# Summing the weighted values of a graph-attention block: accumulating transposes against an fp32 matmul with a stationary identity

## The chip, the cores and the metric

The kernel runs on one core of one Trainium2 chip. The metric is the device time of an execution in microseconds (us), as the median of several runs.

## The reference

Four graph layers are applied in sequence to x (3327 nodes, 256 features, fp32) under an adjacency matrix adj (3327 x 3327, int32, about 0.5% ones). Layer 0 is a simple attention over all nodes. Layers 1, 2 and 3 are the same block with their own weights, 8 heads of 32 features:

```python
qkv = layer_norm(x, g1, be1) @ w_qkv
qkv = qkv.reshape(n, 3, HEADS, HEAD_DIM)
q, k, v = (qkv[:, 0], qkv[:, 1], qkv[:, 2])
scores = jnp.einsum('nhd,mhd->hnm', q, k) * SCALE
scores = jnp.where((adj != 0)[None, :, :], scores, -jnp.inf)
attn = jax.nn.softmax(scores, axis=-1)
out = jnp.einsum('hnm,mhd->nhd', attn, v).reshape(n, DIM)
x = x + out @ w_proj + b_proj
h2 = layer_norm(x, g2, be2)
return x + jax.nn.gelu(h2 @ w1 + b1) @ w2 + b2
```

What matters here is the weighted sum `out`: a node has only some 16 neighbours, and out is the sum over them of (share of the head) times (value row).

## The kernel before, in words

**Layer 0 and the lists.** The first 420 us or so compute layer 0, turn the adjacency into a list of neighbours for each node, and sort the nodes by their number of neighbours into 26 blocks of 128. CAPS gives the slots (places for neighbours) of each block, from 34 for block 0 down to 9 for block 25, 430 in all. None of this is touched by the change.

**A layer.** `layer(L)` runs once for each of layers 1 to 3 under a schedule that is written out by hand: the order in which the Python code issues instructions is the order in each engine's queue. Blocks come in the order 23, 22, ... 0, 24, 25 (ORDER). A block's slots are cut into groups of 3 or 4 (`cuts`); one pass of the inner loop, a *turn*, handles one group. There are 354 turns in three layers. In a turn:

- `gather` issues, up to three groups ahead, one indirect DMA per slot on POOL's queue (L775). It brings for each of the 128 nodes of the block the key and the value row of one neighbour, 2 KB, into a slot tile `sl` (12 tiles of four slots).
- `scores` multiplies the keys by q on DVE (L789) and sums over each head (L790). q lies in a PSUM tile `qp`, which ACT fills in `place_q` (L768). After a block's last group, `exps` and, a turn later, `shares` form the softmax.
- `turn()` advances the *tails* by one step each. A tail is a Python generator for a chunk of two blocks (the last two blocks are chunks of their own): projection (L676), residual, layer norm, the two MLP matmuls (L700, L713) with gelu (L704) between them, and, in layers 1 and 2, the next layer's norm and q, k, v (`qkv_rows`, L182 to L189), whose rows go out by DMA on SP's queue (L739, L740). A number given by `yield` says after how many turns the generator goes on. `hidden` lets only one tail at a time into the MLP.
- `values` works on the block before the current one. DVE multiplies the value half of a group in place by the shares (L822), and PE then adds the group's slots up.

**How the slots are added up.** A slot holds 128 nodes in partitions and 256 features along the free axis, and the projection needs features in partitions. Each slot is therefore turned by two PE transposes (L825), each with the slot's data as the weights and the identity as the moving operand, and all transposes of a block accumulate into one PSUM tile `po` (2 x 128 columns): the sum is already turned. A matmul of zeros (L812) opens the accumulation for both halves at once. When the last group is in, ACT copies po into `oT` (L831), and `part` starts the chunk's tail at the next turn once both of its blocks are there. Behind that copy, in ACT's queue, stands `place_q` for the next block.

**Buffers.** [...]four in the ring `gen` for everything in the tails, two for po, two for qp. In SBUF the pool `work` has two buffers for each tag; the tag `kv` belongs to the k/v rows that `qkv_rows` copies out.

Of the kernel before, what the change touches and what calls it, by code (L numbers as in the profile page):

```python
# [8 lines left out]
FP = mybir.dt.float32  # L9
BF = mybir.dt.bfloat16  # L10
# [8 lines left out]
P = 128  # L19
N = 3327  # L20
D = 256
# [38 lines left out]
CHUNKS = [ORDER[k:k + 2][::-1] for k in range(0, NB - 2, 2)] + [[NB - 2], [NB - 1]]  # L60
# [3 lines left out]
def kernel(ctx: ExitStack, tc: tile.TileContext, ins, out: bass.AP):  # L64
    nc = tc.nc

    def wt(L, name):
        return ins[f"L{L}_gnn_{name}"]

    const = ctx.enter_context(tc.tile_pool(name="const", bufs=1))  # L70
# [3 lines left out]
    ident = const.tile([P, P], FP, name="ident")  # L74
# [2 lines left out]
    nc.vector.tensor_copy(ident_bf, ident)  # L77
    ones = const.tile([P, P], FP, name="ones")
    nc.vector.memset(ones, 1.0)
    zeros_bf = const.tile([1, 2 * P], BF, name="zeros_bf")  # L80
    nc.vector.memset(zeros_bf, 0.0)
    mhalf = const.tile([P, 4], FP, name="mhalf")
    nc.vector.memset(mhalf, -0.5)

# [18 lines left out]
    def load_wq(L):  # L103
        t = wq_pool.tile([P, 2, 3 * D], FP, tag="wq", name=f"wq{L}")
        nc.sync.dma_start(t, wt(L, "w_qkv").rearrange("(c p) n -> p c n", p=P))
        return t
# [87 lines left out]
    def node_rows(b):  # L194

        if b not in nodes_:
            nodes_[b] = lists.tile([P, NODE], FP, tag="node", bufs=NODES, name=f"node_{b}")
        nc.gpsimd.indirect_dma_start(
            out=nodes_[b], out_offset=None, in_=node_dr[:, :],
            in_offset=bass.IndirectOffsetOnAxis(ap=perm[:, b:b + 1], axis=0))  # L200
# [34 lines left out]
    with ExitStack() as st, tc.manual_schedule():  # L235
# [17 lines left out]
        o = 0  # L253
# [33 lines left out]
        for L in LAYERS:  # L287
            o = 16 * (L - 1)
            for k, name in ((0, "g1"), (2, "be1"), (4, "g2"), (6, "be2"), (8, "b1")):
                n = wt(L, name).shape[0] // P  # L290
                nc.sync.dma_start(cols[o + k:o + k + n, :], wt(L, name).rearrange("(c p) -> c p", p=P))
        for L in LAYERS:
            for k, name in enumerate(("b_proj", "b2")):
                r = 2 * (L - 1) + k
# [99 lines left out]
        for i in range(NB):  # L394
            r = ROWS[i]
# [195 lines left out]
        for i in range(NB + 1):  # L591
# [6 lines left out]
            for part, k0 in enumerate(range(0, NB, 8)):  # L598
# [15 lines left out]
                if i:  # L614
                    for k in range(k0, k0 + kn):
                        nc.tensor.matmul(pa[:, :3 * H0 + 1], aTs[i - 1][:, k, :], hs[:, k, :],
                                         start=(k == 0), stop=(k == NB - 1))
# [6 lines left out]
            if i:  # L624
                f, j = in_fin[i - 1]
# [14 lines left out]
    with ExitStack() as st:  # L640
        keep = st.enter_context(tc.tile_pool(name="keep", bufs=1))
        wts = st.enter_context(tc.tile_pool(name="wts", bufs=1))
        work = st.enter_context(tc.tile_pool(name="work", bufs=2))
        slots = st.enter_context(tc.tile_pool(name="slots", bufs=SLOTS))
        ps_g = st.enter_context(tc.tile_pool(name="ps2_g", bufs=4, space=PSUM))
        ps_o = st.enter_context(tc.tile_pool(name="ps2_o", bufs=2, space=PSUM))
        ps_q = st.enter_context(tc.tile_pool(name="ps2_q", bufs=2, space=PSUM))

        def gen(name):
            return ps_g.tile([P, 512], FP, tag="g", name=name)  # L650

        x_sb = keep.tile([P, NB, D], FP, name="x_sb")
        def node_x(b):
            nc.scalar.copy(x_sb[:, b, :], nodes_[b][:, :D])

        def load_weights(L):
            w = {}
            for name, c, n in (("w_proj", 2, D), ("w1", 2, FF), ("w2", 8, D)):
                w[name] = wts.tile([P, c, n], FP, tag=name, name=f"{name}_{L}")
                nc.sync.dma_start(w[name], wt(L, name).rearrange("(c p) n -> p c n", p=P))  # L660
            return w
# [88 lines left out]
        class Attend:  # L750
# [51 lines left out]
            def shares(self):  # L802
                S = self.S
                scs = self.sc[:, :S, :]
                sm = work.tile([P, HEADS], FP, tag="sm", name=f"sm_{self.tag}")
                nc.vector.tensor_reduce(sm, scs.rearrange("p s h -> p h s"), AX.X, ALU.add)
                nc.vector.reciprocal(sm, sm)

                self.pw = self.qp[:, :LW * HEADS].rearrange("p (s h) -> p s h", h=HEADS)
                nc.vector.tensor_mul(self.pw[:, :S, :], scs, sm[:, None, :].to_broadcast([P, S, HEADS]))  # L810
                self.po = ps_o.tile([P, 2, P], FP, tag="po", name=f"po_{self.tag}")
                nc.tensor.matmul(self.po.rearrange("p c r -> p (c r)"), zeros_bf[:, :P], zeros_bf,  # L812
                                 start=True, stop=False)

            def values(self, oT, j):

                g = self.vdone
                a, z = self.cuts[g]
                n = z - a
                t = self.tiles[g]  # L820
                vv = t[:, :n, D:2 * D].rearrange("p s (h d) -> p s h d", h=HEADS)
                nc.vector.tensor_mul(vv, vv, self.pw[:, a:z, :, None].to_broadcast([P, n, HEADS, HD]))  # L822
                for k in range(n):
                    for c in range(2):
                        nc.tensor.matmul(self.po[:, c, :], t[:, k, D + c * P:D + (c + 1) * P], ident,  # L825
                                         is_transpose=True, start=False,
                                         stop=(a + k == self.S - 1 and c == 1))
                self.vdone += 1
                if self.vdone < len(self.cuts):
                    return False  # L830
                nc.scalar.copy(oT[:, :, j * P:(j + 1) * P], self.po)  # L831
                return True

        place = {b: (m, j) for m, blocks in enumerate(CHUNKS) for j, b in enumerate(blocks)}
        tails = []
        hidden = []

        def turn():

            for e in list(tails):  # L840
                e[0] -= 1
                if e[0] <= 0:
                    e[0] = next(e[1], None)
                    if e[0] is None:
                        tails.remove(e)

        def layer(L):
            w = load_weights(L)
            wqn = load_wq(L + 1) if L < LAYERS[-1] else None
            att = [Attend(L, b) for b in ORDER]  # L850
            todo = [(a, g) for a in att for g in range(len(a.cuts))]
            turns = len(todo)
            held = 0
            sent = 0
            oTs = {}
            left = [len(c) for c in CHUNKS]
            first = L == LAYERS[0]
            if first:
                for b in ORDER[:EARLY]:
                    node_rows(b)  # L860
                    node_x(b)
            att[0].load_q()
            att[0].place_q()
            att[1].load_q()
            before = None

            def part(a):

                m, j = place[a.b]
                if m not in oTs:  # L870
                    oTs[m] = work.tile([P, 2, 2 * P], FP, tag="oT", name=f"oT_{L}_{m}")
                if a.values(oTs[m], j):
                    left[m] -= 1
                    if not left[m]:
                        tails.append([1, tail(L, w, wqn, CHUNKS[m], oTs.pop(m))])

            now = 0
            for k, a in enumerate(att):
                n = len(a.cuts)
                if k + 2 < NB:  # L880
                    att[k + 2].load_q()
                for g in range(n):
                    if first and g == 0:
                        if k + EARLY < NB:
                            node_rows(ORDER[k + EARLY])
                        if EARLY <= k + 2 < NB:
                            node_list(ORDER[k + 2])
                            node_x(ORDER[k + 2])
                    while sent < turns and held < SLOTS and sent - now <= AHEAD:
                        todo[sent][0].gather(todo[sent][1])  # L890
                        sent += 1
                        held += 1
                    a.scores(g)
                    if g == n - 1:
                        a.exps()
                    turn()
                    if before is not None:
                        if g == 0:
                            before.shares()
                        goal = -(-len(before.cuts) * (g + 1) // max(n - 1, 1))  # L900
                        while before.vdone < min(goal, len(before.cuts)):
                            part(before)
                            held -= 1
                            if before.vdone == len(before.cuts) and k + 1 < NB:
                                att[k + 1].place_q()
                    elif g == n - 1:
                        att[1].place_q()
                    now += 1
                before = a
            before.shares()  # L910
            while before.vdone < len(before.cuts):
                part(before)
                turn()
            while tails:
                turn()
# [194 lines left out]
```

## Time and profile before

| | |
|---|---|
| Median of 3 runs | 2417.78 us (2409.95 to 2418.01) |
| The profiled execution's own time | 2978.47 us |
| Its span | 2976.6 us |
| Mean granted TensorE clock in it | 0.737 |
| Busy, of the span | PE 60%, DVE 59%, POOL 48%, PEld (weight loads) 46%, ACT 26% |
| DMA | 453.04 MB, mean 152 GB/s; POOL's queue 350.26 MB |

PE is TensorE's matmul side, PEld its weight loads, which overlap with it; DVE is VectorE, ACT ScalarE, POOL GpSimd, SP SyncE. L825 is line 825 of the kernel before. A group line gives line, engine, operation, output<-inputs, shapes and count; after the bar the busy time, the mean length of one in ns, and then the idle time of the engine just ahead of them with what ended it. "issue" is time in which an engine waited for nothing that the profile shows. Durations come from the one profiled execution, which took 561 us longer than the median of the timed runs.

### The profile page before, as it was taken

The page shows a single profiled execution, that of the slowest core. Times are in us where ns is not written, and L with a number is a line of the kernel's source. Part 1 is how long each engine was busy: PE and PEld are TensorE (multiplying, and loading weights), DVE is VectorE, ACT ScalarE, POOL GpSimd, SP SyncE. Part 2 cuts the span into 40 slices and gives each one's busy share as a digit, 9 for nine tenths or more (in the row PEclk, how much of TensorE's full clock was granted, in tenths as well). Part 3 has the DMA queues.
Part 4 walks back from the last instruction along what each step waited for, and adds up shares of the span by engine and source line. Part 5 has one row for each costly group of instructions (what it writes and reads, how often), then busy time and mean ns, then how long its engine had stood idle before and what let it go on. Part 6 is the DMA issues. An engine that isn't in the chain of part 4 may idle for free.

```text
span 2976.6 us, 26066 instructions
## 1 busy us (share of the span) xinstructions
PE 1773.0 (60%) x8346; PEld 1360.5 (46%) x8346; DVE 1769.4 (59%) x3214; ACT 776.9 (26%) x1564; POOL 1426.4 (48%) x1614
## 2 busy tenths in 40 slices
PE   7767632555675556662566665576815656555656
PEld 6545412443454444542445554455614534444545
DVE  6767646655566677715544576657436646665573
ACT  5677410222322222230122221222301221111112
POOL 0221346554445556325544456556164655665651
PEclk9888755677787777785777767778956767667777
DMA  6556275555445556435554456555174554655550
GB/s 237 186 173 196 61 137 167 151 152 148 132 138 164 160 165 181 122 131 161 148 149 132 128 172 187 165 171 171 48 232 120 163 161 129 177 165 157 169 157 24
DMA packets 165082, 453.04 MB, mean 152 GB/s; under 512 B 37711, under 2 KB 64985, under 8 KB 161609
## 3 DMA queue, kind: packets, MB, share of 16 engines
q0 software_dynamic: 107104, 350.26, 41.0%
q1 hardware_dynamic: 57468, 100.88, 11.1%
q8 instruction: 69, 1.13, 0.2%
q14 instruction: 77, 0.63, 0.1%
q10 hardware_dynamic: 364, 0.13, 0.0%
HBM read 410.86 MB, written 40.29 MB: 152 GB/s over the span
## 4 chain that ended last, share of the span: by engine, by line
PE 22%; another core or an unknown queue 11%; issue 10%; DVE 9%; POOL 3%; ACT 3%; DMA 2%; DVEq 0%; POOLq 0%; ACTq 0%
PE pd L713 6%; PE pu L700 6%; PE po L825 4%; POOL sl L775 3%; DVE sl L822 2%; DVE sl L789 2%; DMA sl<-kv,idx 2%; PE pp L676 2%; PE pk L182 2%; DVE sc L790 1%; PE pq L187 1%; DVE st_f L129 1%; DVE x_sb L679 1%; ACT L704 0%
## 5 line engine op out<-in xcount | busy, mean ns | idle before, releaser
L775 POOL DMA_INDIRECT sl<-kv,idx x1290 | 1232.9, 956 | 585.3 <-issue 366.6
L825 PE MATMUL po<-ident,sl 128*128 128x128 f32 x2580 | 482.8, 351 | 543.5 <-DVE sl L822 335.8
L789 DVE TENSOR_TENSOR sl<-sl,qp 128x1024 f32<-128x1024 f32 (+1 forms) x354 | 396.3, 1119 | 561.7 <-ACT qp L768 399.7
L825 PEld LDWEIGHTS po<-ident,sl 128*128 128x128 f32 x2580 | 403.7, 183 | 610.8 <-DVE sl L822 375.8
L700 PE MATMUL pu<-fT,w 128*128 128x256 f32 (+1 forms) x1344 | 345.0, 411 | 116.6 <-issue 93.4
L790 DVE TENSOR_REDUCE sc<-sl 128x32 f32<-128x1024 f32 (+1 forms) x354 | 398.2, 1125 | 17.4 <-DVE sl L789 3.0
L822 DVE TENSOR_TENSOR sl<-sl,qp 128x1024 f32<-128x1024 f32 (+1 forms) x354 | 389.1, 1119 | 4.0 <-DVE qp L810 1.0
L713 PE MATMUL pd<-w,gT 128*128 128x256 f32 x1248 | 324.7, 417 | 100.6 <-ACT gT L704 88.1
L700 PEld LDWEIGHTS pu<-fT,w 128*128 128x128 f32 x1344 | 273.8, 219 | 173.2 <-issue 109.0
L713 PEld LDWEIGHTS pd<-w,gT 128*128 128x128 f32 x1248 | 255.4, 210 | 197.2 <-ACT gT L704 92.7
L182 PE MATMUL pk<-wq,hT 128*128 128x512 f32 x312 | 192.7, 751 | 69.8 <-issue 48.5
L704 ACT ACTIVATE gT<-pu,pv 128x256 f32<-128x256 f32 (+1 forms) x336 | 133.0, 457 | 385.5 <-PE pu L700 164.2
L831 ACT COPY oT<-po 128x256 f32<-128x256 f32 x78 | 29.0, 372 | 754.7 <-PE po L825 359.6
L719 DVE TENSOR_TENSOR x_sb<-x_sb,pd 128x512 f32<-128x512 f32 (+1 forms) x42 | 27.2, 647 | 317.8 <-PE pd L713 247.1
L136 POOL TENSOR_TENSOR rsig_f<-rsig_f,mhalf 128x2 f32<-128x2 f32 (+1 forms) x42 | 29.4, 700 | 383.9 <-DVE rsig_f L132 383.7
L182 PEld LDWEIGHTS pk<-wq,hT 128*128 128x128 f32 x312 | 68.2, 242 | 132.0 <-issue 98.2
L187 PE MATMUL pq<-wq,hT 128*128 128x256 f32 x312 | 90.5, 417 | 61.3 <-ACT kvr L184 50.3
L187 PEld LDWEIGHTS pq<-wq,hT 128*128 128x128 f32 x312 | 67.1, 217 | 115.7 <-issue 55.4
L622 DVE MAX8 cand<-abf 128x8 f32<-128x256 bf16 x338 | 116.6, 411 | 1.9
L676 PE MATMUL pp<-w_proj,oT 128*128 128x256 f32 x312 | 102.1, 481 | 23.2 <-ACT oT L831 20.1
L162 PE MATMUL pn_f<-ident,xn_f 128*128 128x128 f32 x156 | 40.3, 395 | 92.7 <-ACT xn_f L152 69.0
L136 POOL TENSOR_TENSOR rsig_h<-rsig_h,mhalf 128x2 f32<-128x2 f32 (+1 forms) x28 | 19.4, 694 | 157.6 <-DVE rsig_h L132 122.5
(220 smaller groups left out, 1972.8 us busy)
## 6 DMA issues: line engine op xcount, KB each, us to landing
a<-in_adj_dram SPq DMA_DIRECT2D x25, 1663.5 KB
sl<-kv,idx POOLq DMA_INDIRECT x1290
kv<-kvr SPq DMA_DIRECT2D x78, 256.0 KB
q<-qr SPq DMA_DIRECT2D x52, 128.0 KB
q<-q SPq DMA_DIRECT2D x52, 128.0 KB
w<-in_L_gnn_w_dram SPq DMA_DIRECT2D x6, 1024.0 KB
node<-x SPq DMA_DIRECT2D x26, 128.0 KB
node<-qr SPq DMA_DIRECT2D x26, 128.0 KB
```

The costliest lines, as they stand in the source:

```text
L182: nc.tensor.matmul(pk, hT[:, c, :], wq[:, c, D:], start=(c == 0), stop=(c == 1))
L187: nc.tensor.matmul(pq[:, :D], hT[:, c, :], wq[:, c, :D], start=(c == 0), stop=(c == 1))
L622: nc.vector.max(out=cand[:, 8 * m:8 * m + 8], in_=ab3[:, m, :])
L676: nc.tensor.matmul(pp[:, j, :], oT[:, c, j * P:(j + 1) * P], w["w_proj"][:, c, :], start=False, stop=(c == 1 and j == n - 1))
L700: nc.tensor.matmul(pu[:, a, :n * P], w["w1"][:, c, f * P:(f + 1) * P], fT[:, c, :n * P], start=(c == 0), stop=(c == 1))
L704: nc.scalar.activation(gT[:, f0 + a, :n * P], pu[:, a, :n * P], AF.Gelu_apprx_tanh, bias=pv[:, L - 1, 8 + f:9 + f])
L713: nc.tensor.matmul(pd[:, j, :], gT[:, f, j * P:(j + 1) * P], w["w2"][:, h * FH + f, :], start=False, stop=(h == 1 and f == FH - 1 and j == ...
L775: nc.gpsimd.indirect_dma_start(out=t[:, k - a, :w], out_offset=None, in_=kv_dr[self.L][:, :], in_offset=bass.IndirectOffsetOnAxis(ap=idx[: ...
L789: nc.vector.tensor_mul(kq, kq, self.qp[:, None, :D].to_broadcast([P, n, D]))
L790: nc.vector.tensor_reduce(self.sc[:, a:z, :], kq.rearrange("p s (h d) -> p s h d", h=HEADS), AX.X, ALU.add)
L822: nc.vector.tensor_mul(vv, vv, self.pw[:, a:z, :, None].to_broadcast([P, n, HEADS, HD]))
L825: nc.tensor.matmul(self.po[:, c, :], t[:, k, D + c * P:D + (c + 1) * P], ident, is_transpose=True, start=False, stop=(a + k == self.S - 1 ...
```

## The change

The slots of a block are first added up unturned, and the sum is turned once. A matmul with the identity as the stationary operand copies its moving operand to its output; with two slots as the moving operand (2 x 256 = 512 columns) it adds two slots into one PSUM bank, the even ones on the left half and the odd ones on the right. A group of four takes two such matmuls, a group of three one of 512 columns and one of 256. The matmul of zeros goes, since the first matmul of a block opens the accumulation. After a block's last group ACT copies the 512 columns to SBUF (`so`, in the tag `kv`). A new generator `turned_out` joins the tails: at the next turn four transposes turn so and add its two halves into a bank of `gen`, a turn later ACT copies that into oT, and if the block completes its chunk the chunk's tail follows after another turn.

```diff
-    zeros_bf = const.tile([1, 2 * P], BF, name="zeros_bf")
-    nc.vector.memset(zeros_bf, 0.0)
...
-                self.po = ps_o.tile([P, 2, P], FP, tag="po", name=f"po_{self.tag}")
-                nc.tensor.matmul(self.po.rearrange("p c r -> p (c r)"), zeros_bf[:, :P], zeros_bf,
-                                 start=True, stop=False)
+                self.po = ps_o.tile([P, 2 * D], FP, tag="po", name=f"po_{self.tag}")
...
-                for k in range(n):
-                    for c in range(2):
-                        nc.tensor.matmul(self.po[:, c, :], t[:, k, D + c * P:D + (c + 1) * P], ident,
-                                         is_transpose=True, start=False,
-                                         stop=(a + k == self.S - 1 and c == 1))
+                for k in range(0, n, 2):
+                    m = min(2, n - k)
+                    nc.tensor.matmul(self.po[:, :m * D], ident, t[:, k:k + m, D:2 * D],
+                                     start=(a + k == 0), stop=(a + k + m == self.S))
                 self.vdone += 1
                 if self.vdone < len(self.cuts):
                     return False
-                nc.scalar.copy(oT[:, :, j * P:(j + 1) * P], self.po)
+                self.so = work.tile([P, 2 * D], FP, tag="kv", name=f"so_{self.tag}")
+                nc.scalar.copy(self.so, self.po)
                 return True
+
+            def turned_out(self, oT, j, then):
+                po = gen(f"pt_{self.tag}").rearrange("p (c r) -> p c r", c=2)
+                for m in range(2):
+                    for c in range(2):
+                        o = m * D + c * P
+                        nc.tensor.matmul(po[:, c, :P], self.so[:, o:o + P], ident, is_transpose=True,
+                                         start=(m == 0 and c == 0), stop=(m == 1 and c == 1))
+                yield 1
+                nc.scalar.copy(oT[:, :, j * P:(j + 1) * P], po[:, :, :P])
+                if then:
+                    yield 1
+                    yield from then
...
                     left[m] -= 1
-                    if not left[m]:
-                        tails.append([1, tail(L, w, wqn, CHUNKS[m], oTs.pop(m))])
+                    oT = oTs[m] if left[m] else oTs.pop(m)
+                    tails.append([1, a.turned_out(oT, j, None if left[m] else tail(L, w, wqn, CHUNKS[m], oT))])
```

## The prediction

> **What bounds the kernel now.** I read the page first (engine totals, clock slices, chain, groups), then the wait totals, then the timeline of a stretch inside layer 2. On the page:
>
> ```profile
> PE 1773.0 (60%) x8346; PEld 1360.5 (46%) x8346; DVE 1769.4 (59%) x3214; ACT 776.9 (26%) x1564; POOL 1426.4 (48%) x1614
> ...
> PEclk9888755677787777785777767778956767667777
> ...
> PE 22%; another core or an unknown queue 11%; issue 10%; DVE 9%; POOL 3%; ACT 3%; DMA 2%; DVEq 0%; POOLq 0%; ACTq 0%
> ...
> L775 POOL DMA_INDIRECT sl<-kv,idx x1290 | 1232.9, 956 | 585.3 <-issue 366.6
> L825 PE MATMUL po<-ident,sl 128*128 128x128 f32 x2580 | 482.8, 351 | 543.5 <-DVE sl L822 335.8
> ```
>
> No engine is full and the chain has no owner: 21% of it has no releaser (unknown queue, issue). That share is about 613 us; the profiled execution took 2978.5 us (span 2976.6), 560.7 over the median 2417.78. I take that idle to be mostly absent from the timed runs, so I add differences to 2417.78 and trust durations, not gaps.
>
> The timeline (start, length, engine, line, count) gives the real paces:
>
> ```profile
> 1486.95 0.96 POOL L775 DMA_INDIRECT sl<-kv,idx  x1 [0.30 <-issue]
> 1488.22 0.96 POOL L775 DMA_INDIRECT sl<-kv,idx  x1 [0.30 <-issue]
> ...
> 1493.30 0.34 PEld L182 LDWEIGHTS pk<-wq,hT 128*128 128x128 f32 x1 [0.52 <-issue]
> 1494.15 0.34 PEld L182 LDWEIGHTS pk<-wq,hT 128*128 128x128 f32 x1 [0.52 <-issue]
> ```
>
> ```profile
> 1502.75 1.04 PE L825 MATMUL po<-ident,sl 128*128 128x128 f32 x8
> ...
> 1504.06 0.19 PEld L182 LDWEIGHTS pk<-wq,hT 128*128 128x128 f32 x1 [0.24 <-issue]
> 1504.48 0.19 PEld L182 LDWEIGHTS pk<-wq,hT 128*128 128x128 f32 x1 [0.24 <-issue]
> ...
> 1525.94 1.97 PE L825 MATMUL po<-ident,sl 128*128 128x128 f32 x8 [1.97 <-DVE sl L822]
> ```
>
> The reader is to see two things. POOL issues one gather (one slot) every 1.26 us, whatever else stalls. And PE has two speeds: a transpose every 0.109 us at full clock, (1.04 - 0.27)/7, and 0.213 at half clock, (1.97 - 0.48)/7; a 512-column fp32 pass every 0.43 or 0.86 us. The same starts in the trace give 0.216 or 0.427 for a 256-column pass. The mean granted clock is 0.737.
>
> Per block of S slots, outside the layer ends: **POOL** 1.26 S + 0.7 (L136, half a pair's two). **DVE** 0.92 S + 4: L789, L790 and L822 total 1187 us over 1290 slots, softmax pieces 1.8, half a pair's tail 2.2; layer 1 has some 3 more for lists. **PE** at full clock 0.218 S + 11.1: per pair of blocks 32 passes each of L700 and L713 and 8 of L676 at 0.216, four transposes (16.0 us), and for layers 1 and 2 the next q/k/v, 5.6 us; half of that, plus the zeroing matmul L812 at 0.3. At S = 18 this is POOL 23.4, DVE 20.6, PE 15.0. Adding the largest of the three over 78 blocks gives 1708 us at full clock, 1723 at 0.8. With 423 us before the first gather (read from its start) and three layer ends without gathers of about 75 us (1243 to 1318 us is the first), that is 2355 to 2370, 2% under the median. So the gather queue sets the time inside a layer, with DVE and PE close behind in narrow blocks; a serial tail sets it at the ends.
>
> How PE gets onto the path is in the wait totals (total, times, longest):
>
> ```profile
> DVE sl L789 <- ACT qp L768: 399.7, 31, 26.1
> ACT oT L831 <- PE po L825: 359.6, 46, 17.8
> POOL sl L775 <- PE po L825: 83.7, 24, 12.1
> ```
>
> ACT stands in L831 until PE has finished a block's po; the next block's q (L768) is queued behind it, and DVE's scores wait for q. Slots also come free only when PE has read them.
>
> **What the Trainium skill says.** "FP8 and Floating Point Precision", TensorE Precision Notes: true fp32 takes four passes. The trace agrees in time: L700 issues 672 matmuls and shows 1344 records, and 256 columns take 2 x 0.216 us. Transposes have one record each. "TensorE: Matmul & The Clock Gate", Part 1: the clock is half or full, set by activity in windows of about 3.4 us; the trace's clock steps only between 0.5 and 1.0. The same page, Part 4, says that transpose mode does not count as activity; here the clock rises at 1234.6 us after transposes alone since 1230.2, so I don't count on real matmuls waking it.
>
> **The change part by part.**
> 1. *po.* Removed: 2580 transposes, 2580 x 0.109 = 281 us at full clock. Added: 228 groups of four slots take two 512-column matmuls each, 126 groups of three take one and one of 256 columns. At two passes: (456 + 126) x 2 = 1164 passes x 0.429 = 499, and 252 x 0.216 = 54; together 554. Per slot 0.43 instead of 0.218. The trace has no matmul with ident as fp32 weights over a strided pair of slots; the nearest row is L182. Low end: one pass, 277 us, nothing gained or lost. High end: the 0.19 us weight load not covered by the pass before, +1416 x 0.19 = 269. I take two passes, loads covered, as in L182. **+273 us of PE.**
> 2. *Zeroing* (L812, 78 x 0.31) goes: -24 us PE.
> 3. *turned_out*: 4 x 78 transposes x 0.109 = +34 us PE. ACT's copy out of po grows from 0.37 to 0.59 us (L184's shape): +0.22 ahead of the next q; the second copy, 0.37 x 78 = 29 us, runs a turn later. ACT is 26% busy, so apart from the 0.22 this is covered. Queued behind the wait for the turning transposes on ACT are gelu and exp; the transposes have had a turn by then.
> 4. *tail* starts two turns later. Inside a layer the gathers cover that. At the end nothing does.
> 5. *Buffers.* so shares the two kv buffers with L184; it waits for a row write issued a turn before, and in the trace such packets are done 2 to 3 us after issue, so I put it at nothing, upper bound 1.5 us a block, 117 us. pt takes one more of the four gen banks per block: no row prices it; between nothing and the same bound. SP and POOL issue nothing new.
>
> PE per block becomes 0.43 S + 11.2; over three layers 1074 to 1358 us at full clock. **Inside a layer** what counts is where this passes POOL and DVE. S = 11: 15.9 against 14.6; S = 18: 18.9 against 23.4, hidden. Redoing the sum of maxima: +7 us at full clock, +34 at 0.87, +80 at 0.8, +151 at 0.74. The timed clock isn't shown; I expect about 0.8 before and somewhat more after, since PE idles less: **+45**. **At a layer end** block 0's 34 values ran at DVE's pace, 1230.2 to 1241.9 = 11.7 us; 34 passes of 0.429 take 14.6, about 18 with the first 6.8 us at half clock: +6. The last two blocks' 19 slots add 2, their copies and turns 2, the two late turns 2 to 6: **13 a layer, 39 in all**. Sum +84, or 2978.5 + 84 = 3063 for a profiled execution if its idle stayed, and **2500 us** on the median.
>
> **Rivals.**
> - *PE becomes the bound throughout.* Clock 0.74 before and after: +151 +39, or 2608. For: 0.737 in the profile. Against: that clock contains the long unexplained idle.
> - *Hidden.* Clock near full: +7, ends smaller than I think, 2427. For: POOL's steady 1.26. Against: the ends have no gathers to hide behind.
> - *Faster: the clock.* Denser PE work keeps it full where it now drops to half. From 0.74 (sum 1741) to 1 (1715) is -26; with ends at full clock and the zeroing gone, 2395. It decides if the mean clock rises by 0.2 or more. Against: transposes already wake it.
> - *The turn waits.* so or pt holds ACT 1 to 1.5 us a block ahead of q: +117 at most, with half of part 1, about 2545.
> - *One pass only* for the new matmul: then PE is level and only the tail's two turns remain, 2425, counted with "hidden".
>
> **How the numbers follow.** Forecast 50%; PE bound 18%; turn waits 10%; hidden (with one pass) 11%; faster 11%. A measurement of this kernel tells about 0.5% from no change (2406 to 2430). Faster 0.11, same 0.11, slower 0.78. The range 2405 to 2615 leaves out most of the faster case and the top of the PE-bound one.
>
> **What would show it.** Right: po with some 1416 passes of 0.43/0.86 us, PE busy up by 280 us or more at an equal clock, L831's successor waiting longer for po, longer pauses of POOL at layer ends. A profiled execution may even lose part of its idle, as PE issues fewer instructions; the timed runs decide. Wrong: half as many passes; a clock well above 0.8; or POOL's gathers still 1.26 apart through narrow blocks.

## The result, and the profile after

The kernel with the change takes **2483.98 us** (median of 4 runs, 2481.66 to 2490.44) against 2415.81 for the kernel before beside it: a ratio of **1.029 [1.0262, 1.0318]**, or +68 us. Forecast were 2500 us and +84.

The profile of before that the prediction reads holds some 560 us of idle that these runs don't have: on one of the chips used here the unchanged kernel takes some 2969 us (2949 to 2990 in all its runs), with a similar idle inside the layers, and elsewhere 2404 to 2418. So the traces are compared against a second profile of before (experiment e1: 2415.22 us, span 2413.4), which is free of it. Its page:

```profile
PE 1647.3 (68%) x8346; PEld 1290.9 (53%) x8346; DVE 1775.3 (74%) x3214; ACT 782.3 (32%) x1564; POOL 1423.6 (59%) x1614
...
PEclk9888876568887888796778889878957878877777
...
PE 26%; DVE 21%; DMA 15%; POOL 12%; issue 10%; ACT 1%; DVEq 0%; POOLq 0%; ACTq 0%
...
L825 PE MATMUL po<-ident,sl 128*128 128x128 f32 x2580 | 471.5, 346 | 531.3 <-DVE sl L822 530.5
```

And the page of the changed kernel (profiled execution 2490.44 us, span 2488.7). Most of its lines stand two lower than in before: the gathers are L773 (before L775), the power for the norms L134 (L136), the MLP L698 and L711 (L700 and L713), q's copy L766 (L768). New are the summing matmuls L822, the copy L828, the turning transposes L837 and the second copy L840.

```profile
PE 1860.2 (75%) x7416; PEld 1203.1 (48%) x7416; DVE 1775.8 (71%) x3213; ACT 828.5 (33%) x1648; POOL 1424.1 (57%) x1614
...
PEclk9888876689989989996989999899968988888889
...
PE 37%; DVE 16%; issue 13%; POOL 10%; DMA 8%; ACT 2%; DVEq 0%; POOLq 0%; ACTq 0%
...
L773 POOL DMA_INDIRECT sl<-kv,idx x1290 | 1230.2, 954 | 418.2 <-issue 318.3
L822 PE MATMUL po<-sl,ident 128*128 128x512 f32 (+1 forms) x1416 | 727.3, 656 | 408.2 <-DVE sl L818 360.2
```

Fewer PE instructions (7416 for 8346) are busy for longer (1860 us for 1647) although the mean granted clock rose from 0.794 to 0.872. DVE and POOL do what they did, and ACT is busy for 46 us more, with the added copies. PE's share of the chain goes from 26% to 37%.

**Where the time went.** The start of each gather on POOL cuts the trace into parts: a layer runs from its first to its last gather, and its end from there to the next layer's first gather (in layer 3 to the end of the span). The sums are worked out from those starts; us, layers 1, 2, 3:

| | inside the layers | their ends | before the first slot's gather |
|---|---|---|---|
| before (e1) | 605.1, 577.1, 593.2 | 70.8, 71.4, 68.2 | 427.6 |
| after | 620.2, 591.7, 597.0 | 87.1, 86.4, 78.4 | 427.9 |
| difference | +15.1, +14.6, +3.8 = **+33.5** | +16.3, +15.0, +10.2 = **+41.5** | +0.3 |

Together +75, which is the difference of the spans (2488.7 - 2413.4).

**Inside a layer, which blocks?** Layer 2 is cut where block 11, the first of the wider ones, starts its gathers. Each line: window, its length, busy time (instructions) of the engines, granted clock, DMA share, GB/s. Before (e1): narrow blocks, wide blocks, end of the layer.

```profile
1103.50:1322.20 218.70, 139.34 (x622) 109.60 (x623) 162.43 (x233) 60.75 (x117) 163.38 (x173) 0.73 0.74 229
1322.20:1655.10 332.90, 256.94 (x1192) 201.27 (x1191) 273.58 (x377) 96.13 (x194) 243.55 (x260) 0.84 0.71 216
...
1680.60:1752.00 71.40, 60.17 (x290) 45.34 (x288) 23.73 (x60) 27.56 (x65) 4.57 (x8) 0.95 0.13 43
```

After, the same three stretches:

```profile
1135.10:1352.40 217.30, 154.22 (x502) 94.75 (x503) 165.01 (x238) 54.93 (x115) 163.63 (x173) 0.84 0.77 229
1352.40:1702.80 350.40, 299.77 (x1001) 185.20 (x1000) 268.04 (x372) 110.87 (x213) 243.78 (x259) 0.92 0.70 206
...
1726.80:1813.30 86.50, 73.43 (x308) 49.66 (x306) 26.36 (x66) 30.86 (x71) 5.29 (x9) 0.98 0.11 37
```

The narrow stretch did not grow (218.7 and 217.3); the wide one grew by 17.5 us, and there PE is now busy for 300 of 350. Cut at the same block, layer 1 shows the same (-4.3 and +19.6) and layer 3 little (+2.7 and +0.9). Part of the reason that PE is fuller beside the wide blocks is where the MLP matmuls run. In after, of layer 2's passes of L698:

```profile
1135.10:1352.40 217.30, 25.32 (x112) 0.84 0.77 229
```

The tails lag their blocks, so only 112 of 448 passes fall beside the twelve narrow blocks; and the clock rises there, from 0.73 to 0.84. That alone does not explain why the narrow blocks got off free: in before (e1) the tails lag as well, with 117 passes (L700) in the same stretch. The experiments e3 and e4 come back to it.

**How PE's work stops the gathers.** POOL computes one thing in a tail, the power of the norm (L134), and it does so in its place in the queue of gathers. Timeline of after, in layer 2's wide stretch (start, length, engine, line; in brackets the idle before it and its releaser):

```profile
1614.50 0.95 POOL L773 DMA_INDIRECT sl<-kv,idx  x1 [0.30 <-issue]
...
1615.46 3.62 PE L711 MATMUL pd<-w,gT 128*128 128x256 f32 x16
...
1619.12 0.69 DVE L717 TENSOR_TENSOR x_sb<-x_sb,pd 128x512 f32<-128x512 f32 x1 [0.57 <-PE pd L711]
...
1621.05 0.17 DVE L130 TENSOR_SCALAR rsig_h<-mv_h 128x2 f32<-128x2 f32 x1
...
1621.39 0.71 POOL L134 TENSOR_TENSOR rsig_h<-rsig_h,mhalf 128x2 f32<-128x2 f32 x1 [5.94 <-DVE rsig_h L130]
...
1622.30 1.02 POOL L773 DMA_INDIRECT sl<-kv,idx  x1 [0.19 <-issue]
```

DVE's residual and statistics wait for PE to finish pd, and so POOL stands for 5.94 us at the power, and no gather starts for 7.8 us (1614.50 to 1622.30) instead of 1.26. POOL's waits within layer 2 (total, times, longest), before (e1):

```profile
POOL rsig_h L136 <- DVE rsig_h L132: 12.5, 4, 5.0
...
POOL rsig_f L136 <- DVE rsig_f L132: 9.1, 3, 3.9
```

and after:

```profile
POOL rsig_h L134 <- DVE rsig_h L130: 24.5, 7, 5.9
...
POOL rsig_f L134 <- DVE rsig_f L130: 12.4, 4, 6.0
```

21.6 us have become 36.9: +15.3, where the layer grew by 14.6.

### The profile page after: what moved, and what is told of

Same layout as the page of the kernel before. It is cut to its first block, busy times and chain, and to the rows that moved or that the text cites. A ratio compares the mean times of both kernels' runs of the same rounds, so it can differ in the third digit from the quotient of the medians.

```text
span 2488.7 us, 24576 instructions
## 1 busy us (share of the span) xinstructions
PE 1860.2 (75%) x7416; PEld 1203.1 (48%) x7416; DVE 1775.8 (71%) x3213; ACT 828.5 (33%) x1648; POOL 1424.1 (57%) x1614
## 4 chain that ended last, share of the span: by engine, by line
PE 37%; DVE 16%; issue 13%; POOL 10%; DMA 8%; ACT 2%; DVEq 0%; POOLq 0%; ACTq 0%
PE po L822 13%; POOL sl L773 8%; PE pu L698 7%; PE pd L711 7%; DMA sl<-kv,idx 7%; PE pk L180 4%; DVE sl L787 3%; DVE sl L818 3%; DVE sc L788 3%; PE pp L674 2%; PE pq L185 2%; DVE st_f L127 1%; DVE x_sb L677 1%; POOL out_dram L722 1%; PE pt L837 1%
## 5 line engine op out<-in xcount | busy, mean ns | idle before, releaser
L773 POOL DMA_INDIRECT sl<-kv,idx x1290 | 1230.2, 954 | 418.2 <-issue 318.3
L822 PE MATMUL po<-sl,ident 128*128 128x512 f32 (+1 forms) x1416 | 727.3, 656 | 408.2 <-DVE sl L818 360.2
L822 PEld LDWEIGHTS po<-sl,ident 128*128 128x128 f32 x1416 | 305.1, 224 | 716.3 <-DVE sl L818 387.0
L711 PE MATMUL pd<-w,gT 128*128 128x256 f32 x1248 | 288.4, 383 | 11.4 <-ACT gT L702 11.4
L698 PE MATMUL pu<-fT,w 128*128 128x256 f32 (+1 forms) x1344 | 284.8, 365 | 2.0 <-ACT fT L162 2.0
L698 PEld LDWEIGHTS pu<-fT,w 128*128 128x128 f32 x1344 | 241.2, 191 | 47.0 <-issue 13.2
L711 PEld LDWEIGHTS pd<-w,gT 128*128 128x128 f32 x1248 | 232.3, 190 | 57.4 <-ACT gT L702 17.1
L828 ACT COPY so<-po 128x512 f32<-128x512 f32 x78 | 45.7, 586 | 634.2 <-PE po L822 399.1
L182 ACT COPY kvr<-pk 128x512 f32<-128x512 f32 x78 | 45.6, 585 | 204.5 <-PE pk L180 204.3
L134 POOL TENSOR_TENSOR rsig_f<-rsig_f,mhalf 128x2 f32<-128x2 f32 (+1 forms) x42 | 29.6, 704 | 133.9 <-DVE rsig_f L130 133.4
L150 ACT ACTIVATE xn_f<-x_sb,nmu_f,rsig_f 128x256 f32<-128x256 f32 x78 | 42.8, 593 | 165.0 <-DVE nmu_f L146 151.3
L602 ACT ACTIVATE aT<-pt 128x1024 bf16<-128x1024 bf16 x104 | 87.1, 861 | 16.9 <-PE pt L601 16.1
L601 PE MATMUL pt<-ident_bf,abf 128*128 128x128 bf16 x676 | 60.3, 232 | 37.8 <-ACT aT L602 37.8
```

The source lines that it names most:

```text
L601: nc.tensor.transpose(pt[:, m, :], abfs[i][:, (k0 + m) * P:(k0 + m + 1) * P], ident_bf)
L602: nc.scalar.activation(aTs[i][:, k0:k0 + kn, :], pt[:, :kn, :], AF.Sign)
L698: nc.tensor.matmul(pu[:, a, :n * P], w["w1"][:, c, f * P:(f + 1) * P], fT[:, c, :n * P], start=(c == 0), stop=(c == 1))
L711: nc.tensor.matmul(pd[:, j, :], gT[:, f, j * P:(j + 1) * P], w["w2"][:, h * FH + f, :], start=False, stop=(h == 1 and f == FH - 1 and j == ...
L773: nc.gpsimd.indirect_dma_start(out=t[:, k - a, :w], out_offset=None, in_=kv_dr[self.L][:, :], in_offset=bass.IndirectOffsetOnAxis(ap=idx[: ...
L822: nc.tensor.matmul(self.po[:, :m * D], ident, t[:, k:k + m, D:2 * D], start=(a + k == 0), stop=(a + k + m == self.S))
```

## The experiments

Experiments e1 to e4 ran on a chip where the kernel before takes 2408.48 us (11 runs). e5 to e8 ran on a chip where it takes 2968.79 us (26 runs), and e9 to e12 on the same chip beside 2970.13 us (22 runs). What was expected of e5 to e12 was written for the first chip, so the times in us are all missed; ratios and differences are read instead, and where these were missed too, it is said.

**e1: the kernel before again**, unchanged, for a profile.

> The kernel before, unchanged, for a second profile. Theory A (PE load is the cost of the change; the first profile's 561 us over the timed runs are idle that the timed runs don't have): a profile near 2416 us is possible, with the pauses between a layer's last gather and the next layer's first near the 75 us of the first profile and a mean clock of 0.8 to 0.87. Rival (the long idle belongs to this program whenever it is profiled): again 2950 us or more.

Measured: 2415.22 us, span 2413.4, clock 0.794. The long idle of the first profile is gone; lines and sums are above.

**e2: less PE work in the sum.** The summing matmuls read the upper 16 bits of each value, against a bf16 identity; the rest is the changed kernel.

```diff
-                    nc.tensor.matmul(self.po[:, :m * D], ident, t[:, k:k + m, D:2 * D],
+                    hi = t[:, k:k + m, D:2 * D].bitcast(BF).rearrange("p s (d two) -> p s d two", two=2)[:, :, :, 1]
+                    nc.tensor.matmul(self.po[:, :m * D], ident_bf, hi,
```

> The changed kernel, with the summing matmuls on the upper 16 bits of each value (bf16 identity): what is left out is the values' lower 16 bits. One pass instead of two[...]: 582 passes of 0.216 us and 126 of 0.109 are 139 us of PE instead of 554; the copies, the turn and its lateness stay. Theory A (PE load): 39 us inside the layers and part of the ends go, 2420 to 2440. Theory B (the turn: copy, four transposes, copy and tail two turns later): still 2470 to 2485. Theory C (shared buffers): as B.

Measured: 2401.73 us, **0.9968 [0.9955, 0.9981]**. From its page:

```profile
L823 PE MATMUL po<-sl,ident_bf 128*128 128x512 bf16 x708 | 265.4, 473 | 663.6 <-DVE sl L818 603.0
```

708 records for 708 matmuls, where fp32 leaves 1416: one pass instead of two. Each pass is shorter too: at full clock, passes of 512 columns start 0.227 us apart instead of 0.429. The sum thus takes about a quarter of the PE time that it takes in after, and about half of what it takes in before. With copies, turns and late tails all still there, this takes away the whole loss, more than theory A expected. The parts differ, though: layers 588.9, 562.9, 591.3 (32 us shorter than before), ends 81.0, 79.7, 73.4 (24 us longer).

**e3: PE work alone.** The kernel before, each transpose of a slot issued twice (so that each slot is counted twice); no copy, no turn, no late tail.

```diff
-                        nc.tensor.matmul(self.po[:, c, :], t[:, k, D + c * P:D + (c + 1) * P], ident,
-                                         is_transpose=True, start=False,
-                                         stop=(a + k == self.S - 1 and c == 1))
+                        for twice in range(2):
+                            nc.tensor.matmul(self.po[:, c, :], t[:, k, D + c * P:D + (c + 1) * P], ident,
+                                             is_transpose=True, start=False,
+                                             stop=(a + k == self.S - 1 and c == 1 and twice == 1))
```

> The kernel before, with each transpose issued twice (so the attention sum is doubled): 2580 more of 0.109 us are 281 us more PE at full clock, as many as the change adds, and no turn. Theory A: 2455 to 2475. Theory B and C: 2416 to 2425.

Measured: 2476.63 us, **1.0296 [1.0271, 1.0322]**, +68, as the change itself. It adds 2580 x 0.109 = 281 us of PE at full clock; the change adds 273 - 24 + 34 = 283.

```profile
L826 PE MATMUL po<-ident,sl 128*128 128x128 f32 x5160 | 729.6, 306 | 406.5 <-DVE sl L822 406.1
```

That PE work alone costs this much is shown. That it equals the total of the change is partly chance: here layers grow by 52 us (632.9, 599.3, 595.3) and ends by 13 (76.2, 76.6, 70.4), against 33.5 and 41.5.

**e4: no late turn.** The changed kernel, with the four transposes, the copy into oT and the tail's start all at the first turn after the block.

```diff
                                          start=(m == 0 and c == 0), stop=(m == 1 and c == 1))
-                yield 1
                 nc.scalar.copy(oT[:, :, j * P:(j + 1) * P], po[:, :, :P])
                 if then:
-                    yield 1
                     yield from then
+                yield None
```

> The changed kernel, with the four transposes, the copy into oT and the tail's first step all at the turn after the last group, as early as the tail starts in the kernel before. Theory A: only the late start is saved, a few us a layer end, less what PE now waits for ACT inside the turn: 2465 to 2485. Theory B: 2420 to 2440. Theory C: 2475 to 2485.

Measured: 2519.97 us, **1.0469 [1.0451, 1.0486]**: +111 us, where the change has +68 beside its own kernel before, against every theory. Ends are 79.1, 79.7, 74.2, or 19 us shorter than after's, as hoped; layers are 642.2, 620.7, 595.7, or 50 longer. The waits of e4, all three layers, have one that after doesn't:

```profile
PEld pp L674 <- ACT oT L839: 50.2, 42, 3.8
```

The projection now follows its transposes in PE's queue at once and stands there for ACT's copy; what is queued behind it stands too. POOL's waits within e4's layer 1:

```profile
POOL rsig_f L134 <- DVE rsig_f L130: 33.1, 7, 9.7
POOL rsig_h L134 <- DVE rsig_h L130: 18.2, 6, 8.8
```

51.3 us, where after's layer 1 has 36.1. So the late turn is not a mere loss: it saves time inside a layer and costs at the ends.

**The five kernels together.** POOL's idle just ahead of the power, summed over layers 1 and 2 from the trace, beside the time inside them:

| layers 1 + 2, us | e2 | e1 (before) | after | e3 | e4 |
|---|---|---|---|---|---|
| POOL idle ahead of the power | 18.1 | 41.9 | 73.0 | 82.3 | 109.3 |
| against before | -23.8 | | +31.1 | +40.4 | +67.4 |
| time inside the layers | 1151.8 | 1182.2 | 1211.9 | 1232.2 | 1262.9 |
| against before | -30.4 | | +29.7 | +50.0 | +80.7 |

The two go together in all five. In layer 3, which has one norm per chunk instead of two and no next q, k, v, the five lie within 6 us. The same two quantities by stretch, again for layers 1 and 2 together (here with the shortest gaps counted in, which adds up to 0.7 us):

| layers 1 + 2, us | e1 (before) | after | e3 | e4 |
|---|---|---|---|---|
| narrow blocks (23 to 12), length | 450.9 | 445.2 | 470.2 | 480.7 |
| of it, POOL idle ahead of the power | 10.5 | 5.1 | 29.8 | 40.3 |
| wide blocks (11 to 0), length | 679.6 | 716.7 | 701.0 | 718.6 |
| of it, POOL idle ahead of the power | 32.1 | 68.4 | 53.0 | 69.2 |

In each stretch the length grows about as much as this wait does. (The last two blocks, not in the table, add 9 us in e3 and 12 in e4, by gathers that wait themselves.) In e3 the narrow blocks lose as much as the wide ones, although the clock in their stretch of layer 2 is 0.84, as in after, and 112 MLP passes fall there as well. In after they lose nothing, and in e4, which is after without the late turns, they lose again. So it is the late turns that spare the narrow blocks in after. How they do that these runs don't show.

If the power's wait is what carries PE's lateness into the gathers, then asking for the power later should shorten the layers:

**e6, e10 and e7, e11: powers later.** The changed kernel (e6, repeated as e10) and the kernel before (e7, repeated as e11), with two turns instead of one between the statistics and the power, except while the last two blocks run (`late[0]` starts at 2). The edit is the same in both:

```diff
             mv, rs = variances(views, f"f{tag}")
-            yield 1
+            yield late[0]
             powers(rs, n)
...
             mv, rs = variances(views, f"h{tag}")
-            yield 1
+            yield late[0]
...
+                late[0] = 2 if k < NB - 2 else 1
```

> The changed kernel, with POOL's power (line 134) issued one turn later in all but the last two blocks of a layer, so that it no longer stands in POOL's queue waiting for DVE and PE with gathers behind it. Theory A2 (inside a layer the change costs only through this wait, 73 us of POOL idle in layers 1 and 2 against 42 in the kernel before): most of it goes, 2420 to 2445. Theory A1 (PE is the bound of narrow blocks, or holds the slots): 2470 to 2485.

> The kernel before with the same shift. Theory A2: its 42 us of POOL waiting at that line go too, 2365 to 2385. Theory A1: no change, 2405 to 2416.

Measured against the kernel before on the same chip: before with late powers **0.9643 [0.961, 0.9675]** and **0.9718 [0.9693, 0.9743]**; after with late powers 0.9876 [0.9843, 0.9909] and 0.9842 [0.9811, 0.9874]. For the repeats, theory A2 had expected ratios of 0.985 to 0.990 (e11) and 1.005 to 1.015 (e10) on the first chip; both came out lower on this one, where the power's wait is longer. In e7's profile the layers take 767, 724 and 730 us, where the first profile of before has 816, 772 and 739: 106 less; POOL's idle ahead of the power falls by 95, from 400 to 305 in all three (e11: 86 and 84 less). That the in-order power costs gather time is shown by this edit, on the chip with the long idle; on the other it rests on the table. The change still costs something with powers late, 2932.13 / 2867.13 = 1.023 in the first pair and 2926.04 / 2887.46 = 1.013 in the second; the two disagree by more than their intervals allow, so its size is left open. Theory A2, that the change costs inside a layer only through the power's wait, does not hold there. In e6 POOL waits less at the power than in e7 (276 us against 306 inside the layers), and yet the layers are 25 us longer in all (e10 against e11: 21), while the gathers themselves now wait longer for PE to have read their slots. In e7 and e6:

```profile
POOL sl L775 <- PE po L825: 57.2, 24, 12.7
```

```profile
POOL sl L773 <- PE po L822: 121.2, 38, 11.8
```

In the repeats these are 54.4 and 130.0 us. With one wait shortened, the change's PE work reaches the gathers by another. The ends are 25 and 30 us longer.

**e5, e9: lateness alone.** The kernel before, with every tail started two turns later.

```diff
-                        tails.append([1, tail(L, w, wqn, CHUNKS[m], oTs.pop(m))])
+                        tails.append([3, tail(L, w, wqn, CHUNKS[m], oTs.pop(m))])
```

> The kernel before, with each tail starting two turns later, nothing else. It prices the lateness alone. Theory A (PE load inside the layers, lateness at their ends): the pauses at the layer ends grow by 15 to 20 us in all of the 24 that the bf16 kernel still shows, inside a layer nothing: 2423 to 2430. Rival (the lateness itself relieves the layers, as the no-late kernel's longer layers could mean): layers shorter by 20 to 40 us, 2385 to 2410.

Measured: 1.0031 [1.0012, 1.0051] and, repeated, 1.0011 [0.9998, 1.0024]. Ends are 9 us longer in all (79.9, 80.5, 71.2, against 74.8, 74.4, 73.3 in the first profile of before), where 15 to 20 were expected. Inside the layers nothing is reproducible: 25 us shorter in e5's profile, 16 longer in e9's.

**e8, e12: less PE work than before has.** The kernel before, but DVE writes the weighted values as bf16, and PE sums and turns each slot by two bf16 matmuls of one pass; e12 adds the late powers.

```diff
-                nc.vector.tensor_mul(vv, vv, self.pw[:, a:z, :, None].to_broadcast([P, n, HEADS, HD]))
+                vb = t[:, :n, :D // 2].bitcast(BF)
+                nc.vector.tensor_mul(vb.rearrange("p s (h d) -> p s h d", h=HEADS), vv,
+                                     self.pw[:, a:z, :, None].to_broadcast([P, n, HEADS, HD]))
...
-                        nc.tensor.matmul(self.po[:, c, :], t[:, k, D + c * P:D + (c + 1) * P], ident,
-                                         is_transpose=True, start=False,
+                        nc.tensor.matmul(self.po[:, c, :], vb[:, k, c * P:(c + 1) * P], ident_bf, start=False,
```

> The kernel before, with DVE writing the weighted values in bf16 (rounded, into the key half of the slot) and PE turning and adding them in one pass each by plain bf16 matmuls, the data as weights and a bf16 identity moving; no late turn. What is left out is precision of the values below bf16. If a bf16 pair costs about 0.1 us like the transpose, PE load is as before: 2395 to 2412. If PE load falls with the cheaper weight load, POOL's waits fall towards the 18 us of the other bf16 kernel and the ends stay short: 2375 to 2395.

> The kernel before with the weighted values in bf16 (left out is their precision below bf16), turned and added by bf16 matmuls of one pass, and POOL's power one turn later. A bf16 pass had 0.056 us between starts at full clock and 0.107 at half, the fp32 transpose 0.109 and 0.213, so PE falls by about 140 us at full clock. Theory A2: with the power shifted there is no POOL wait left for it to shorten, so it is level with the kernel with the shift alone, to within 0.3%, or gains up to 10 us at the layer ends: ratio 0.980 to 0.990. Theory A1: PE relief gains inside the layers as well: below 0.980.

Measured: e8 2949.29 us, **0.9918 [0.989, 0.9947]**; e12 2862.02, **0.9639 [0.9613, 0.9664]**. PE's lighter sum gives 0.8% alone. With the late powers, e12 is 0.9% faster than e11 (2887.46 us), which ran beside it, and level with e7 of the earlier runs (2867.13 us). Since e7 and e11 are one kernel and lie 0.7% apart, what the lighter sum adds then stays open; that e12 is below 0.980, theory A1's sign, decides nothing, because e11 is so without it. In fp32 the late powers in the kernel before (e7, e11) are the fastest version that ran on that chip. The changed kernel alone was not run there, nor the late powers on the other chip.

## Why the prediction was right, and where it was not

**PE's work: right.** Each fp32 matmul is two passes, 1416 records, 429 or 854 ns apart for 512 columns at full and half clock and 216 or 427 for 256. The strided pair of slots costs nothing extra, and weight loads are covered. e3 adds the same PE time and costs the same; e2 takes away three quarters of the sum's PE time and the loss is gone.

**The clock: right.** Estimated "about 0.8 before and somewhat more after"; 0.794 and 0.872. Whether 0.872 is the "clock well above 0.8" that was to be a sign of being wrong, the prediction does not settle. The faster rival needed a rise of 0.2 and got 0.08.

**Inside the layers, +45: measured +33.5. Size fair, mechanism wrong.** At a clock of 0.87 its own sum gives +34, but that this meets the measured +33.5 is luck, because other blocks pay than it said, and in another way. The step that failed is the one "where this passes POOL and DVE. S = 11: 15.9 against 14.6; S = 18: 18.9 against 23.4, hidden". It charged each block its own tail, 11.2 us of PE spread evenly, and expected the loss in narrow blocks. The windows show none there (-1.4 us in layer 2) and all of it in the wide ones (+17.5). e3 shows that PE work by itself would have cost the narrow blocks too; what spared them is the late turns, which the prediction put at nothing inside a layer. Nor is the price that PE's sum passes POOL's: it is a wait. The 0.7 us a block for L136 was put into POOL's sum as work, without asking what the power itself waits for. In layers 1 and 2 POOL stands ahead of it for 73.0 us, before 41.9, and those 31 us are the 30 by which the layers grew.

The wait could be seen beforehand. The prediction read that POOL issues a gather every 1.26 us, "whatever else stalls". In the wait totals of the first profile, the row just below the first one that it shows is

```profile
POOL rsig_f L136 <- DVE rsig_f L132: 383.7, 34, 24.1
```

and in the timeline from which it took the paces stands

```profile
1514.35 0.72 POOL L136 TENSOR_TENSOR rsig_f<-rsig_f,mhalf 128x2 f32<-128x2 f32 x1 [20.11 <-DVE rsig_f L132]
```

that is, 20 us without a gather. This also explains much of why its sum for the kernel before, 1708 to 1723 us, lies 52 to 67 under the 1775 that the layers of e1 take: POOL stands at the power for 42 of them. "POOL's gathers still 1.26 apart through narrow blocks" was named as a sign of being wrong; for this step, it was.

**Ends, +39: measured +41.5.** In layer 1, counted from the last gather, before and after: block 0's po copied at -0.9 and 6.6, the first projection at -0.9 and 16.3, the first MLP matmul at 21.8 and 38.0, the next gather at 70.8 and 87.1. So 7.5 us is PE's sum (predicted 6 to 8), and 9.7 the copy and the late turns (predicted 4 to 8); of these 17.2 us, 16.3 arrive at the next layer's first gather. The chain in after's timeline:

```profile
1047.01 7.03 PE L822 MATMUL po<-sl,ident 128*128 128x512 f32 x16
...
1048.10 0.95 POOL L773 DMA_INDIRECT sl<-kv,idx  x1 [0.30 <-issue]
...
1054.12 0.59 ACT L828 COPY so<-po 128x512 f32<-128x512 f32 x1 [17.17 <-issue]
...
1054.76 0.66 PE L837 MATMUL pt<-ident,so 128*128 128x128 f32 x4 [0.72 <-ACT so L828]
...
1056.68 0.36 ACT L840 COPY oT<-pt 128x256 f32<-128x256 f32 x1
...
1064.43 1.99 PE L674 MATMUL pp<-w_proj,oT 128*128 128x256 f32 x8
```

and before (e1), where the projection follows the copy at once:

```profile
1031.39 0.37 ACT L831 COPY oT<-po 128x256 f32<-128x256 f32 x1 [14.60 <-PE po L825]
...
1031.81 2.00 PE L676 MATMUL pp<-w_proj,oT 128*128 128x256 f32 x8
```

oT is complete at 1057.0, but its tail's next turn comes with another block's summing in front, and the projection starts at 1064.4. After against e2 gives the split of all three ends: 251.9 - 234.1 = 17.8 us for the PE time that e2 takes away, 234.1 - 210.4 = 23.7 for the rest.

**The late turn "inside a layer": covered, and worth more than nothing.** e5 and e9 show no cost, in the kernel before and on the other chip; e4 shows that without it the changed kernel's layers are 50 us longer.

**Buffers, nothing: borne out.** All 78 copies into so (L828) start within 0.1 us of the end of their block's last pass, so none waited for its buffer, and no large wait on the tag gen appears. The wait that does, PE's for so (L837: 31.0 us on PE over 43 times, longest 0.7), is the price of turning soon after the copy and is inside the numbers above.

**The idle of the first profile.** Adding differences to the median was right; calling the idle "mostly absent from the timed runs" held for these. It is not confined to profiled executions, though: on one chip the kernel has a similar idle in all its runs.

**The rivals.** PE bound throughout, 2608: the mean clock rose, and about three quarters of PE's 283 us stayed hidden. Hidden, 2427: the measured loss is 68 us. The turn waits, 2545: no such wait. One pass only: excluded by the records; e2 shows what it would have been, 0.3% faster.

## What to carry to other kernels

Ask of every instruction in a queue that feeds DMAs what it waits for, not only how long it runs: a 0.7 us power in POOL's queue stood 73 us for its inputs with gathers behind it, and asking for it one turn later gained the kernel before some 3% on the chip where that was run, as much as the new sum lost on the other. Comparing the engines' sums block by block misses such a wait; cutting the trace into stretches and reading the idle of the pacing engine in each finds it. When one wait goes, look for the next: with the power late, the changed kernel's gathers waited for slots. A pipeline's lateness, hidden inside a loop, is paid in full at each end of the loop.

## What the runs showed of the hardware

**Transposes raise the clock.** The Trainium skill, "TensorE: Matmul & The Clock Gate", Part 4, says of transpose mode that "it doesn't count as PE-busy the same way". In e3 the only added PE work is transposes, and the mean granted clock went from 0.794 to 0.878, as high as with 1416 fp32 passes (0.872). For these fp32 transposes the measurement disagrees and decides.

**One program, two times.** The same kernel takes 2408 us on one chip and 2969 on another, in 11 and 26 runs. The first profile of before shows the same long form. Ahead of the first gather (427 us) and at the ends (223 us in all there, 210 here) they are nearly alike in it and in e1; the difference lies in the stretches with gathers, 2327 us against 1775. What delays them is not settled: for 11% of its chain, the first profile names "another core or an unknown queue" as what ended the wait. A change's ratio need not carry over between the two; the changed kernel alone was not run on the slower chip.
